# A graph convolution with residual and layer norm: which block of the first stage goes without a tile of g

## The chip, the cores and the metric

The kernel runs on one core of one Trainium2 chip. The metric is the device time of the program in microseconds, as the median of several executions. One more execution was recorded by the hardware profiler; every duration and every view in this document comes from such a profiled execution.

## The reference

The inputs are x (8 x 4096 x 256), a square matrix A (4096 x 4096, sparse and denser towards its first rows and columns) and a weight W (256 x 256), all float32. What is computed, cut to what matters:

```python
HW = jnp.einsum('bnf,fo->bno', H, W)                 # H is x
A_norm = jax.nn.relu((A + A.T) * 0.5)
D = jnp.sum(A_norm, axis=1)
d_inv_sqrt = jnp.where(D > 0, D_safe ** (-0.5), 0.0)
DAD = d_inv_sqrt[:, None] * A_norm * d_inv_sqrt[None, :]
L_norm = jnp.eye(N) - DAD
out = relu(jnp.einsum('nm,bmo->bno', L_norm, HW))
x = layernorm(x + out)                               # over the last axis
```

## The kernel before, in words

The kernel has two stages on the one core. The first stage makes two arrays in device memory: `a_dram`, the symmetrised and clipped matrix, and `g_dram`, the rows of x times W, each scaled by its node's r = D^(-1/2). The second stage gathers, for each pair of row tiles of the result, only the rows of these two arrays that are needed, multiplies them on the tensor engine (PE), and adds the residual and the layer norm.

The change is in the first stage. The matrix is cut into 8 x 8 blocks of 512 x 512, and the two loops run over the upper triangle: for row i from 0 to 7, for column j from i to 7. Off the diagonal a block (i, j) means two tiles, (i, j) and (j, i); on the diagonal one. So there are 36 blocks with 64 tiles. For each block the kernel

- loads the tiles, 1 MB each, on the queue of SyncE (SP), line 486, into a pool `adj` of four buffers;
- transposes the partner tile on PE in 16 pieces per tile (`symmetrise`, L496, tile `tr`) and adds it to the tile itself on VectorE (DVE), four additions per tile (L500, tile `sym`, a pool of three buffers);
- in `keep`, halves and clips the tile on ScalarE (ACT, L504), sums it in groups of 32 columns on DVE (L507, `sums`) and again (L512, `part`), notes on GpSimd (POOL, L508) which groups are not zero, and stores it into `a_dram` from ACT's queue (L513).

The tile (i, j) is spoken of as the first of the block and (j, i) as the second.

Beside most blocks stands one tile of g. There are 32 of them, of 128 nodes each. `form(m)` makes one: it loads x for these nodes in two halves (`xin`, L589 on SP's queue, or L555 on POOL's for rows 4 and up), transposes them on PE (L596, `xtr`), copies them out of PSUM on ACT (L597, `xt`), multiplies by W on PE (L607, `pg`) and scales by r on ACT while leaving PSUM (L617, `gt`). Then it stores the tile (L622) and has a small strip of `a_dram` loaded for it (`fetch`, POOL's queue). `multiply` uses both in the next block for the result's first row tile (L565, `lead`, 16 products).

A tile whose r is not known yet is kept unscaled: the last ten tiles (22 to 31) are made that way, one ahead of the loops and the others in rows 0 and 1. All others wait until `degrees(i)` at the end of a row has given r for the four tiles of that row; they stand in a list `known`. How many tiles of g a block takes is what `quota(i, j)` says: one off the diagonal, one on the diagonal from row 4 on, none on the diagonals of rows 0 to 3. Row 2 has six blocks, (2,2) to (2,7). At its start `known` holds tiles 4 to 7, and the ten early ones are used up. So blocks (2,3), (2,4), (2,5) and (2,6) take tiles 4, 5, 6 and 7, and (2,7) finds nothing to take, although its quota is one. Block (3,3), which follows, has a quota of none; (3,4) takes tile 8.

PSUM has eight banks: four belong to `lead` throughout the stage, and four (`b0`) turn over between the transposes, the tiles of g and the counts of the lists.

A third kind of work is spread over rows 2 to 5: the lists of which rows the second stage will gather (`patterns`, `count_place`, `more`, `count_place_rest`, later `spread_early` and `collect_index`). It is almost all small operations on DVE. A list `due` says after how many tiles each step comes; `run_due` counts down once for every tile kept. In row 2 these steps fall beside blocks (2,2) to (2,6), for the first of the second stage's units.

The order of instructions on each engine is not written by hand. The program gives the work in the order of the loops, and a scheduler in the framework puts it in an order per engine, by the operations' dependencies and its own estimate of their lengths. Each engine then runs its instructions in that order.

Of the kernel before, what the change touches and what calls it, by code (L numbers as in the profile page):

```python
# [67 lines left out]
def kernel(  # L68
# [402 lines left out]
    with (  # L471
# [175 lines left out]

        def quota(i, j):

            if i in (2, 3) and j == i:  # L650
                return 0
            return int(j > i or i > 3)

# [45 lines left out]
        for i in range(NS):  # L699
            diag = stat1.tile([P, A, P], F32, tag="diag", name=f"diag_{i}")  # L700
            for j in range(i, NS):
                tij = load_adj(i, j)
                tji = load_adj(j, i) if j > i else tij
                parts = [(i, j, tij, tji)] + ([(j, i, tji, tij)] if j > i else [])
                parts = [(p, spool.tile([P, A, S], F32, tag="sym", name=f"sym_{p[0]}_{p[1]}")) for p in parts]
                beside = [multiply(*args) for args in waiting]
                waiting.clear()
                products = len(beside)

                for _ in range(quota(i, j)):  # L710
                    if known:
                        beside.append(form(known.pop(0), True, i >= 4))
                    elif early:
                        beside.append(form(early.pop(0), False))
                for p, sym in parts:
                    for _ in symmetrise(*p, sym):
                        pass
                if i == NS - 1:


                    release_all(i - 1)
                    beside = beside[products:] + beside[:products]
                for n, b in enumerate(beside):
                    with tc.issue_after(done_pe[-1]) if i == NS - 1 and n < 2 else nullcontext():
                        for _ in b:
                            pass
                for (rows, cols, _, _), sym in parts:
                    keep(rows, cols, sym, diag)
                    run_due()
# [610 lines left out]
```

## Time and profile before

| | |
|---|---|
| median of three executions | 1734.53 us (1728.11 to 1739.32) |
| profiled execution, its own time | 1485.62 us |
| its span, first to last instruction | 1483.5 us |
| mean granted clock of PE | 0.975 |
| PE busy in the span | 1381.0 us, 93% |
| DVE busy | 1042.3 us, 70% |
| ACT busy | 361.0 us, 24% |
| bytes moved by DMA | 541.85 MB, 365 GB/s |
| PE busy in the first 560 us | 513.81 us |

The profiled execution is 249 us shorter than the median of the others. Its rows give the durations; its own time is what a sum of such durations is to be held against.

A row of a timeline reads: start in us from the beginning of the span, length in us, engine (PEld is the weight load of PE, and a q behind the name is the engine's queue), line, operation, what is written and read, the number of instructions merged into the row, and in brackets the idle time of the engine before it with what ended it. A row of a table by windows gives the stretch, its length, then the busy time of PE, PEld, DVE, ACT and POOL with the number of instructions, the granted clock of PE, the busy share of the DMA engines and the rate in GB/s.

### The profile page before, as it was taken

What the parts mean: (1) busy time and instruction counts of PE and PEld (TensorE: products, weight loads), DVE (VectorE), ACT (ScalarE), POOL (GpSimd) and SP (SyncE); (2) the same over time, 40 slices, a digit from 0 to 9 for tenths busy, and PEclk for the clock granted to TensorE, in tenths of its full rate; (3) what the DMA queues carried; (4) which work ended last, traced back from release to release, by engine and by line L of the source; (5) the groups of instructions that cost most, each with busy time, mean ns of one, the idle gap of its engine ahead of it and who ended that gap; (6) DMA issues with size and microseconds to landing.
All of it is one profiled execution on the core that took longest, in us unless ns stands there. A gap on an engine that the chain in (4) does not pass through costs nothing. (4 is left out here: it accounts for less than half of the span.)

```text
span 1483.5 us, 29574 instructions
## 1 busy us (share of the span) xinstructions
PE 1381.0 (93%) x10960; PEld 750.6 (51%) x10960; DVE 1042.3 (70%) x3174; ACT 361.0 (24%) x462; POOL 762.0 (51%) x1556
## 2 busy tenths in 40 slices
PE   7998988979999998999999999999989999988995
PEld 6777877757777773343433333333333344433432
DVE  4668569879687862219485897798889229999655
ACT  4555554434544460000101101101100010011111
POOL 2445010010223336775775767777777657677752
PEclk9999999999999999999999999999999999999997
DMA  9999999999999999999999999999999989999995
GB/s 347 365 370 385 402 363 360 387 384 328 352 361 349 370 387 377 391 400 334 368 381 359 375 396 367 392 387 378 347 379 386 401 293 360 334 346 400 394 364 188
DMA packets 216694, 541.85 MB, mean 365 GB/s; under 512 B 19070, under 2 KB 108862, under 8 KB 182110
## 3 DMA queue, kind: packets, MB, share of 16 engines
q0 software_dynamic: 55200, 282.68, 49.4%
q1 hardware_dynamic: 93200, 126.62, 24.7%
q10 hardware_dynamic: 68144, 130.58, 23.2%
q8 instruction: 89, 1.46, 0.4%
q14 instruction: 61, 0.50, 0.1%
HBM read 434.91 MB, written 136.34 MB: 385 GB/s over the span
## 5 line engine op out<-in xcount | busy, mean ns | idle before, releaser
L1175 PE MATMUL py<-g,ga 64*32 64x512 f32 (+1 forms) x7072 | 610.4, 607 | 24.5 <-DMA g<-g_dram,gi 24.2
L1175 PEld LDWEIGHTS py<-g,ga 64*32 64x32 f32 (+1 forms) x7072 | 226.9, 114 | 391.5 <-issue 313.9
L952 POOL DMA_INDIRECT ga<-a_dram,ai x265 | 287.6, 1085 | 134.0 <-PE py L1175 67.2
L960 POOL DMA_INDIRECT g<-g_dram,gi x265 | 294.0, 1110 | 112.2 <-issue 72.2
L768 ACT ACTIVATE y<-py,minus_r 128x512 f32<-128x512 f32 x120 | 72.7, 688 | 788.9 <-PE py L1175 570.0
L607 PE MATMUL pg<-w_sb,xt 128*128 128x256 f32 x1024 | 230.2, 384 | 4.3 <-ACT xt L597 4.3
L1175 PE MATMUL py<-g_hub,gh 128*128 128x512 f32 x496 | 229.5, 606 | 3.7 <-DVE pos_k L240 3.7
L607 PEld LDWEIGHTS pg<-w_sb,xt 128*128 128x128 f32 x1024 | 195.3, 193 | 30.4 <-ACT xt L597 5.0
L500 DVE TENSOR_TENSOR sym<-tr,adj 128x512 f32<-128x512 f32 x256 | 162.7, 682 | 58.4 <-PE tr L496 40.9
L507 DVE TENSOR_REDUCE sums<-sym 128x64 f32<-128x2048 f32 x64 | 145.3, 2279 | 62.4 <-ACT sym L504 62.4
L1175 PEld LDWEIGHTS py<-g_hub,gh 128*128 128x128 f32 x496 | 91.5, 191 | 136.2 <-issue 124.2
L496 PE MATMUL tr<-ident,adj 128*128 128x128 f32 x1024 | 136.2, 280 | 21.0 <-DVE sym L500 14.6
L504 ACT ACTIVATE sym<-sym 128x2048 f32<-128x2048 f32 x64 | 122.6, 1915 | 113.6 <-DVE sym L500 107.5
L508 POOL TENSOR_SCALAR uses<-sums 128x64 uint8<-128x64 f32 x64 | 24.8, 388 | 239.4 <-DVE sums L507 203.7
L496 PEld LDWEIGHTS tr<-ident,adj 128*128 128x128 f32 x1024 | 115.3, 143 | 53.5 <-DVE sym L500 32.5
L443 DVE TENSOR_SCALAR low<-lists 128x17 f32<-128x17 f32 (+8 forms) x14 | 2.5, 176 | 197.4 <-PE lists L431 197.4
L778 DVE TENSOR_TENSOR xr<-xr,y 128x2048 f32<-128x2048 f32 x31 | 70.9, 2286 | 54.6 <-ACT y L768 43.1
L596 PE MATMUL xtr<-ident,xin 128*128 128x128 f32 x512 | 72.9, 291 | 20.6 <-DVE sym L500 12.0
L811 DVE TENSOR_SCALAR xr<-xr,mv,root 128x256 f32<-128x256 f32 x248 | 85.8, 417 | 1.1
L787 DVE BATCH_NORM_STATS2 stats<-xr 128x6 f32<-128x256 f32 x248 | 84.0, 412 | 1.1
L565 PE MATMUL lead<-gt,strip 128*128 128x512 f32 x176 | 83.2, 594 | 0.0
L597 ACT COPY xt<-xtr 128x512 f32<-128x512 f32 x128 | 68.2, 592 | 59.2 <-PE xtr L596 57.6
(157 smaller groups left out, 1060.2 us busy)
## 6 DMA issues: line engine op xcount, KB each, us to landing
adj<-in_adj_dram SPq DMA_DIRECT2D x64, 1024.0 KB, 10.5
a_dram<-sym ACTq DMA_DIRECT2D x64, 1024.0 KB, 10.1
out_dram<-xr SPq DMA_DIRECT2D x31, 1024.0 KB, 25.1
xr<-in_x_dram ACTq DMA_DIRECT2D x28, 1024.0 KB, 20.4
xin<-in_x_dram SPq DMA_DIRECT2D x44, 512.0 KB, 11.1
g_dram<-gt ACTq DMA_DIRECT2D x22, 1024.0 KB, 9.4
xin<-in_x_dram POOLq DMA_DIRECT2D x20, 512.0 KB
g_dram<-held ACTq DMA_DIRECT2D x10, 1024.0 KB, 10.2
```

What stands on the lines that cost most here:

```text
L496: ins = nc.tensor.transpose(pt[:, c * P : (c + 1) * P], tji[:, c, a * P : (a + 1) * P], ident)
L500: nc.vector.tensor_add(sym[:, a, :], pt, tij[:, a, :])
L504: nc.scalar.activation(sym, sym, AF.Relu, scale=0.5)
L507: nc.vector.tensor_reduce(sums, sym.rearrange("p a (c q) -> p a c q", q=E), AX.X, ALU.add)
L565: nc.tensor.matmul(lead[c], lhsT=strip, rhs=g[:, c * S : (c + 1) * S], start=not done, stop=len(done) == NB - 1, skip_group_check=True,)
L596: nc.tensor.transpose(pt[:, k, c, :], xin[b // H][:, b % H + k, c * P : (c + 1) * P], ident)
L607: ins = nc.tensor.matmul(pg[:, k * FO : (k + 1) * FO], lhsT=xt[:, b + k, c, :], rhs=w_sb[:, c, :], start=(c == 0), stop=(c == FC - 1),)
L787: nc.vector.bn_stats(stats[:, b, :], z[:, b, :])
L811: nc.vector.tensor_scalar(z[:, b, :], z[:, b, :], mv[:, b, 0:1], rstd[:, b : b + 1], ALU.subtract, ALU.mult,)
L952: nc.gpsimd.indirect_dma_start(out=at if both else at[:, : E if one else P], out_offset=None, in_=a_pairs if both else a_groups if one els ...
L960: nc.gpsimd.indirect_dma_start(out=gt, out_offset=None, in_=g_dram, in_offset=bass.IndirectOffsetOnAxis(ap=gi[:, t : t + 1], axis=0), boun ...
L1175: return nc.tensor.matmul(py[2 * u + 1 + b][c][cols, :], lhsT=at[ps, off + cols.start : off + cols.stop], rhs=gt[ps, c * S : (c + 1) * S], ...
```

## The change

`quota` now names three blocks of rows 2 and 3 that take no tile of g: (2,2), (2,5) and (3,3). The two on the diagonal had none before. Block (2,5) is the fourth of row 2. With it left out, tile 6 goes to (2,6) and tile 7 to (2,7), so every tile of row 2 is still made in that row; the products of `lead` for each tile come one block later as well.

```diff
         def quota(i, j):

-            if i in (2, 3) and j == i:
+            if (i, j) in ((2, 2), (2, 5), (3, 3)):
                 return 0
             return int(j > i or i > 3)
```

## The prediction

> **What bounds the kernel now.** I read the page first, then the first stage by windows, then the stretch around the moved step as timelines of PE, VectorE (DVE) and ScalarE (ACT). A row carries no block number: blocks are told apart by counting rows in the built order.
>
> ```profile
> span 1483.5 us, 29574 instructions
> ...
> PE 1381.0 (93%) x10960; PEld 750.6 (51%) x10960; DVE 1042.3 (70%) x3174; ACT 361.0 (24%) x462; POOL 762.0 (51%) x1556
> ...
> DMA  9999999999999999999999999999999989999995
> ...
> a_dram<-sym ACTq DMA_DIRECT2D x64, 1024.0 KB, 10.1
> ```
>
> PE is busy for 93% of the span, and the DMA engines are at nine tenths or more in 38 of the 40 slices. The last row is a price used below: one store of a symmetrised tile takes 10.1 us from issue to landing. The first stage is the stretch up to some 560 us; seven windows of 80 us give PE 513.81 us of it. It is bound by PE and DMA together, so a moved step can only win where one of them stands still. The windows, with columns PE, PEld, DVE, ACT, POOL, granted clock, DMA share and GB/s, find one such place:
>
> ```profile
> 260.00:280.00 20.00, 18.80 (x107) 14.76 (x106) 19.26 (x49) 9.20 (x11) 1.10 (x3) 1.00 1.04 379
> 280.00:300.00 20.00, 20.00 (x113) 15.60 (x112) 14.06 (x29) 10.64 (x12) 0.73 (x2) 1.00 1.05 400
> 300.00:320.00 20.00, 11.15 (x65) 9.48 (x64) 17.29 (x28) 7.19 (x6) 5.39 (x12) 0.85 1.01 383
> ```
>
> From 300 to 320 us PE has 11.15 us of work in 20: that is 8.9 us lost. It is where block (2,7), which has no tile of g, meets (3,3), which has none either. Note too that DVE has 19.26 of 20 in the window where the change wants to put the light block. PE in that place:
>
> ```profile
> 297.63 2.74 PE L565 MATMUL lead<-gt,strip 128*128 128x512 f32 x6
> 300.21 1.91 PE L496 MATMUL tr<-ident,adj 128*128 128x128 f32 x16
> 307.77 3.95 PE L496 MATMUL tr<-ident,adj 128*128 128x128 f32 x20 [5.65 <-DMA adj<-in_adj_dram]
> 312.71 1.25 PE L496 MATMUL tr<-ident,adj 128*128 128x128 f32 x8 [0.99 <-DVE sym L500]
> 316.10 0.66 PE L496 MATMUL tr<-ident,adj 128*128 128x128 f32 x4 [2.13 <-DVE sym L500]
> 316.82 3.40 PE L596 MATMUL xtr<-ident,xin 128*128 128x128 f32 x16
> 320.01 2.34 PE L607 MATMUL pg<-w_sb,xt 128*128 128x256 f32 x8
> ```
>
> The waits are 5.65 + 0.99 + 2.13 = 8.77 us. The 5.65 has two causes within 0.2 us of each other: the second tile of (3,4), whose load was issued at 297.83 when (2,7) gave its buffer back, and DVE, which runs its queue in order:
>
> ```profile
> 300.85 0.69 DVE L500 TENSOR_TENSOR sym<-tr,adj 128x512 f32<-128x512 f32 x1 [0.99 <-PE tr L496]
> 301.46 4.46 DVE L507 TENSOR_REDUCE sums<-sym 128x64 f32<-128x2048 f32 x2
> ...
> 310.31 0.69 DVE L500 TENSOR_TENSOR sym<-tr,adj 128x512 f32<-128x512 f32 x1 [1.30 <-DMA a_dram<-sym]
> ```
>
> After a block without a tile of g, the two sums of that block (4.46 us) stand in front of the next block's additions, which free the PSUM banks; and the next-but-one tile needs the sym buffer whose store was issued at 299.87 and is released at 310.2. These two are the price of any light block.
>
> **The change part by part.** Nothing is removed or added: 32 tiles of g, the same bytes, the same buffers. Block (2,5) gives up tile 6, which goes to (2,6); tile 7 goes from (2,6) to (2,7). Per tile moved: 16 transposes L596 (1.91 us), 32 products L607 (7.07), 4 copies L597 and 4 scalings L617 on ACT, two xin loads on SP's queue, one g store on ACT's, one strip load on POOL's, and 16 lead products L565 in the next block (some 2.6 us of PE beside the transposes). The PE time in play is 1.91 + 7.07 = 9.0 us.
>
> *What goes.* The 8.77 us at 302 to 317: with tile 7's 9.0 us between (2,7) and (3,3), the loads of (3,4) go out at about 297 and land by 307, ahead of need, and DVE does (2,7)'s first sum under the products.
>
> *What comes, first at (2,6).* PE reaches it at 268.7 (end of the lead products), with 9.0 us fewer in front. DVE is not ready: the two sums of (2,5) end at 272.9 (268.44 + 4.47 in its timeline) and the small ones after them at 273.1, so (2,6)'s first four additions run 273.1 to 275.5. Its second tile needs the sym buffer of (2,5)'s first tile. In the built order that store is no longer behind the four xt copies, so it goes out right after the second relu starts, 268.1 (it was 270.68). With 10.1 us it lands at 278.2. Additions 278.4 to 280.9; the L596 transposes need the banks that these free and end at 281.5; L607 ends at 288.6. Then (2,7) begins at 288.7; before it was 293.2. So of 9.0 us the light block yields 4.5 and 4.5 is lost waiting.
>
> *At (2,7).* DVE now has list work in front: sum of (2,6) to 283.1, the list group (273.08 to 277.4 before, 4.3 us) to 287.5, the scan L236 that waits for PE's count at 288.9, the other sum (2.28) and small ones to 292.0. The additions take 5.8 us as before, to 297.8; tile 7's transposes end at 298.4, its products at 305.5.
>
> *At (3,3) and (3,4).* (3,3) on PE 305.5 to 307.6, lead to 310.2, (3,4) to some 314.6. The second relu of (2,7) stands behind the third scaling in ACT's order, near 304.5, so its store goes out at 306.5 and lands at 316.6. The second tile of (3,4) takes that buffer: its additions start at 316.6 where they started at 316.1. Tile 8's products start at 320 to 322 (a sum of 2.28 us stands between its additions in the new order); before, 320.0. Sum: 0 to +2, taken as **+1 us**.
>
> *Other queues.* SP: tile 7's second xin now stands behind the load for (3,3), which waits for (2,6)'s buffer, about 281; it lands near 291 and is wanted at 296. POOL: the strips of 6 and 7 are the same small loads, later; the degree work of row 2 (L524 to L536, some 2.5 us of DVE with the wait for POOL) now stands ahead of (3,3)'s additions, but under tile 7's products; without that cover it would cost 2.5. Beyond (3,4) the same instructions stand in nearly the same order, so the shift is carried on or absorbed.
>
> *Rule against row, the store.* The Trainium skill, "DMA: Bandwidth & Descriptors", section "Anatomy of one DMA — SWDGE (gpsimd) path", gives a DMA 2.0 us plus bytes over 436 GB/s (a fit for the other kind of queue): an estimate of 4.4 us for 1 MB. By it the store at 268.1 is in before it is wanted, (2,7) starts about 2.9 us sooner, the last store lands near 308, and tile 8's products start near 314.5: **-5.5 us**. The row says 10.1, and 299.87 to 310.2 in this very place, since both queues are full. I take the row.
>
> *Rule against row, the clock.* "TensorE: Matmul & The Clock Gate", section "HAM oscillation", says that idle gaps over some 3.4 us throttle PE. The rows agree: after a gap of 2.13 us (210.5 to 212.6) the 10 us window shows 1.00, after one of 4.03 (228.2 to 232.2) 0.83, and the window with the 5.65 us gap 0.85. By the rule, splitting this gap into waits near 3 us (276.1 to 279.1, and 314.6 to 317.3) would save the slow rows, at most 3.40 - 1.91 = 1.5 us, and the row L596 is also held by DVE. Bounds 0 and -1.5; I take 0, since both waits are close to the limit.
>
> *Bounds.* At best all 8.8 us of the old wait go and nothing comes: -8.8. At worst the 9.0 us uncovered at (2,6) are wholly lost and the old waits return at (3,4): +9.0.
>
> **Own time and the median.** The profiled execution took 1485.62 us (span 1483.5 and 2.1 around it); with the change 1486.6. The median shown is 1734.53, 1.168 times as long, and no view tells where these 249 us lie. If all stretch alike, +1 is +1.2, so **1735.7**, and the bounds are -10.3 and +10.5: within 1% (17.3 us, about what a measurement of this kernel can tell from no change) on both sides.
>
> **The rivals.**
> 1. *The gap is really closed.* Stores land in 4 to 7 us because the light block leaves the queues emptier. For it: SP issues nothing between 270.7 and 282.2. Against it: DMA share 1.04 there. Gain 5.5 to 8.8, times 1.168: **1724 to 1728**.
> 2. *VectorE becomes the bound* (slower). Place: (2,6) and (2,7), where it has 19.26 of 20 us already. Price: the 4.5 us still won at (2,6) are lost there, and the waits for stores come on top at (3,4), 4 to 9 us in all, times 1.168: **1739 to 1745**. It decides when stores land later than some 12 us or list work shifts further ahead of (2,7)'s additions. More than 1% slower needs the unprofiled runs to lose twice what the profile bounds.
> 3. *Waits in the unprofiled runs are much longer than here.* They are 249 us slower; if that time sits in first-stage waits, the same move could weigh 18 us or more either way. For it: nothing here excludes it. Against it: one block of 36.
> That the change does not do what it says is ruled out by the built order: tile 6's products stand after (2,6), tile 7's after (2,7).
>
> **How the numbers follow.** Forecast (-2 to +4 us): 0.45. Rival 1: 0.15. Rival 2: 0.15. Rival 3: faster 0.11, slower 0.14. So faster over 1% 0.11, within 1% 0.75, slower over 1% 0.14. The bounds give 1724 to 1745; the three runs lie 6.4 below and 4.8 above their median, and a second median scatters as well, so I add half as much again: 1714 to 1753. The forecast's own range is 1732 to 1740.
>
> **What would show it.** Right: PE's gap at 302 to 308 gone; a wait of some 6 us in all between 268.7 and 281.5; (2,7) from near 289; a second wait for a_dram<-sym on DVE near 316; tile 8's L607 at 320 to 322. Wrong: L607 of tile 8 before 317 (rival 1) or after 325 (rival 2); or a difference in the runs that the profiled spans don't show (rival 3).

## Result, and the profile after

The changed kernel took 1744.34 us (median of 22 runs, 1729.64 to 1756.44) against 1739.53 us for the kernel before on the same chip (22 runs, 1723.78 to 1754.55). The ratio is 1.002, with an interval of 0.9999 to 1.0041: no difference that these runs can tell from none, and at most some 7 us of loss. The forecast was a loss of 1.2 us.

Executions of these kernels lie on one of two levels, a short one of 1476 to 1488 us or a long one of 1712 to 1756 us, and the first trace of the kernel before is from the short level, the trace of the changed kernel from the long one:

```profile
span 1741.2 us, 29571 instructions
...
PE 1460.2 (84%) x10960; PEld 739.0 (42%) x10960; DVE 1042.2 (60%) x3174; ACT 361.2 (21%) x462; POOL 748.2 (43%) x1556
...
DMA  9999999999999996867777979779778668669984
```

DVE and ACT did the same work as before to 0.2 us. The DMA row shows where the two traces part: its nines, which ran through the first 32 slices before, end after 15 slices of 43.5 us, at 653 us, some 65 us behind the end of the first stage. So all comparisons of traces below are made inside the first stage, where the levels do not differ; the second stage is taken up further down.

The first stage by windows, in the changed kernel:

```profile
260.00:280.00 20.00, 13.41 (x71) 10.10 (x70) 16.60 (x29) 5.81 (x4) 0.75 (x3) 0.81 1.03 384
280.00:300.00 20.00, 19.97 (x111) 16.44 (x110) 17.70 (x47) 10.81 (x14) 1.04 (x2) 0.94 0.95 334
300.00:320.00 20.00, 17.07 (x100) 13.13 (x99) 15.20 (x28) 10.09 (x11) 5.42 (x12) 1.00 1.04 393
```

The hole from 300 to 320 us is gone: PE works 17.07 us there, not 11.15. But 260 to 280 fell from 18.80 to 13.41. Over the 60 us PE is busy 50.45 us, against 49.95 before, and gets through 282 instructions, against 285. The hole was not closed, it was moved and split. PE's timeline names the parts:

```profile
267.91 1.91 PE L496 MATMUL tr<-ident,adj 128*128 128x128 f32 x16
273.01 3.67 PE L496 MATMUL tr<-ident,adj 128*128 128x128 f32 x16 [3.18 <-DVE sym L500]
278.89 3.67 PE L596 MATMUL xtr<-ident,xin 128*128 128x128 f32 x16 [2.21 <-DVE sym L500]
282.36 7.12 PE L607 MATMUL pg<-w_sb,xt 128*128 128x256 f32 x32
...
298.35 7.07 PE L607 MATMUL pg<-w_sb,xt 128*128 128x256 f32 x32
...
315.13 1.25 PE L596 MATMUL xtr<-ident,xin 128*128 128x128 f32 x8 [0.73 <-DVE sym L500]
318.52 1.38 PE L596 MATMUL xtr<-ident,xin 128*128 128x128 f32 x8 [2.13 <-DVE sym L500]
319.74 8.76 PE L607 MATMUL pg<-w_sb,xt 128*128 128x256 f32 x32
```

The figures in brackets are the idle times: 3.18 + 2.21 + 0.73 + 2.13 = 8.25 us, where the old place had 8.77. The three L607 rows are tiles 6, 7 and 8. And DVE, on which all four waits end:

```profile
267.64 4.46 DVE L507 TENSOR_REDUCE sums<-sym 128x64 f32<-128x2048 f32 x2
...
272.28 2.47 DVE L500 TENSOR_TENSOR sym<-tr,adj 128x512 f32<-128x512 f32 x4
278.14 2.48 DVE L500 TENSOR_TENSOR sym<-tr,adj 128x512 f32<-128x512 f32 x4 [3.40 <-issue]
...
314.38 1.29 DVE L500 TENSOR_TENSOR sym<-tr,adj 128x512 f32<-128x512 f32 x2 [0.69 <-PE tr L496]
315.59 2.28 DVE L507 TENSOR_REDUCE sums<-sym 128x64 f32<-128x2048 f32 x1
317.78 0.68 DVE L500 TENSOR_TENSOR sym<-tr,adj 128x512 f32<-128x512 f32 x1
```

The first row holds the two sums of the light block (2,5), in front of the additions that free PE's banks; the third is the second tile of (2,6), 3.40 us late with DVE idle. The view gives no releaser for it ("issue"); what it waited for was settled by an experiment. The last three rows stand at (3,4): a sum of 2.28 us lies between the additions of its second tile, and PE waits its 2.13 us for the ones behind that sum. The kernel before has such a sum in this place too, at 313.17, and the same wait of 2.13.

### The profile page after: what moved, and what is told of

Its sections match the earlier page's. It is cut to its first block, busy times and chain, and to the rows that moved or that the text cites. A ratio compares the mean times of both kernels' runs of the same rounds, so it can differ in the third digit from the quotient of the medians.

```text
span 1741.2 us, 29571 instructions
## 1 busy us (share of the span) xinstructions
PE 1460.2 (84%) x10960; PEld 739.0 (42%) x10960; DVE 1042.2 (60%) x3174; ACT 361.2 (21%) x462; POOL 748.2 (43%) x1556
## 3 DMA queue, kind: packets, MB, share of 16 engines
q0 software_dynamic: 55200, 282.68, 43.5%
## 4 chain that ended last, share of the span: by engine, by line
PE 56%; another core or an unknown queue 12%; DVE 12%; DMA 9%; issue 5%; ACT 2%; POOL 2%; ACTq 0%; DVEq 0%; POOLq 0%
PE py L1175 39%; PE pg L607 8%; DMA a_dram<-sym 5%; PE tr L496 3%; DVE sym L500 3%; PE xtr L596 3%; PE lead L565 3%; DVE sums L507 1%; DMA ga<-a_dram,ai 1%; DVE stats L787 1%; DMA xin<-in_x_dram 1%; DVE xr L811 1%; POOL g L960 1%; POOL ga L952 1%
## 5 line engine op out<-in xcount | busy, mean ns | idle before, releaser
L1175 PE MATMUL py<-g,ga 64*32 64x512 f32 (+1 forms) x7072 | 682.5, 667 | 215.2 <-ACTq L1210 194.6
L1175 PEld LDWEIGHTS py<-g,ga 64*32 64x32 f32 (+1 forms) x7072 | 210.4, 120 | 669.2 <-ACTq L1210 357.4
L952 POOL DMA_INDIRECT ga<-a_dram,ai x265 | 273.2, 1031 | 279.6 <-PE py L1175 216.1
L607 PE MATMUL pg<-w_sb,xt 128*128 128x256 f32 x1024 | 230.5, 384 | 4.3 <-ACT xt L597 4.3
L607 PEld LDWEIGHTS pg<-w_sb,xt 128*128 128x128 f32 x1024 | 195.3, 193 | 30.9 <-ACT xt L597 5.0
L596 PE MATMUL xtr<-ident,xin 128*128 128x128 f32 x512 | 77.0, 301 | 23.7 <-DVE sym L500 16.9
L565 PE MATMUL lead<-gt,strip 128*128 128x512 f32 x176 | 83.6, 595 | 0.0
```

The source lines that it names most:

```text
L565: nc.tensor.matmul(lead[c], lhsT=strip, rhs=g[:, c * S : (c + 1) * S], start=not done, stop=len(done) == NB - 1, skip_group_check=True,)
L596: nc.tensor.transpose(pt[:, k, c, :], xin[b // H][:, b % H + k, c * P : (c + 1) * P], ident)
L607: ins = nc.tensor.matmul(pg[:, k * FO : (k + 1) * FO], lhsT=xt[:, b + k, c, :], rhs=w_sb[:, c, :], start=(c == 0), stop=(c == FC - 1),)
L952: nc.gpsimd.indirect_dma_start(out=at if both else at[:, : E if one else P], out_offset=None, in_=a_pairs if both else a_groups if one els ...
L1175: return nc.tensor.matmul(py[2 * u + 1 + b][c][cols, :], lhsT=at[ps, off + cols.start : off + cols.stop], rhs=gt[ps, c * S : (c + 1) * S], ...
```

## Experiments

Places in the first stage are counted from the start of the L607 products of tile 5 or of the last tile of g in row 1 (both lie ahead of the block (2,5)), so that a small shift at the start of a trace does not count. The expectations call that last tile of row 1 "tile 3"; by the order of the loops it is tile 31, one of those kept unscaled, and its way out of PSUM is the copy to `held` and not L617. It is the same place in every kernel, so no figure changes; below it is tile 31. The stage ends with the last product of `lead`. The four kernels of each of the first two comparisons ran once each with a profile; those of the third were timed as well, 14 to 22 times.

### The two kernels again

> The kernel before, profiled once more. It is to tell what of the difference between the two traces is scatter. From the start of tile 3's products (the last tile of g of row 1, the same in both kernels) the first trace has 105.0 us to the start of tile 8's products and 367.5 us to the end of the first stage. The theory (light block's gain is eaten by waits, nothing else is touched) expects 105 within 1 us again; for the end of the stage, scatter of some 5 us. The rival (the change delays the later rows as well) expects 367.5 within 2. The whole span: near 1740 us, as every timed run, not 1483.5 as in the first trace.

> The changed kernel, profiled once more. First trace: 105.5 us from tile 3's products to tile 8's, 373.2 us to the end of the first stage. The theory expects 105.5 within 1 us, and an end of the stage that falls within the scatter of the kernel before. The rival (the later rows are delayed by the change) expects 373 within 2, 5 to 6 us over the kernel before.

The kernel before took 1712.92 us and the changed one 1725.36; both on the long level. A third trace of the changed kernel came with the timed runs below. In us:

| | tile 5 to 6 | 5 to 7 | 5 to 8 | tile 8 to 9 | tile 8's 32 products | 31 to end of stage |
|---|---|---|---|---|---|---|
| before, first trace | 17.38 | 33.20 | 66.92 | 16.83 | 7.52 | 367.46 |
| before, again | 17.40 | 33.21 | 66.47 | 17.05 | 7.74 | 369.71 |
| changed, first trace | 30.09 | 46.08 | 67.46 | 19.10 | 8.76 | 373.17 |
| changed, again | 30.26 | 46.50 | 68.20 | 19.10 | 8.76 | 375.92 |
| changed, timed | 28.95 | 45.65 | 67.60 | 19.31 | 8.97 | 369.33 |

The two traces of before, one from each level, agree within 0.45 us up to tile 8: so up to there the levels make no difference. Tile 8 comes 0.5 to 1.7 us later with the change, as forecast. The next step, to tile 9, is 2.1 to 2.5 us longer in all three traces, which was not forecast. The rest of the stage, from tile 9 to its end, took 245.6 and 248.1 us in the kernel before and 248.6, 248.8 and 244.2 in the changed one: there the two cannot be told apart.

### The store that the second tile of (2,6) waits for

The store of (2,5)'s first tile is left out, and its place in `a_dram` is written with (5,2)'s, the second tile of the same block; the matrix that the second stage reads is therefore not the right one in that block. The number of bytes stays the same. (In this kernel the lines behind `keep` are numbered 5 higher.)

```diff
-            nc.scalar.dma_start(a_dram[...i, j...], sym)
+            if (i, j) != (2, 5):
+                nc.scalar.dma_start(a_dram[...i, j...], sym)
+            if (i, j) == (5, 2):
+                nc.scalar.dma_start(a_dram[...j, i...], sym)
```

> The changed kernel, with one thing taken away: the store of (2,5)'s first tile reads the second tile's buffer instead (same bytes, same place in memory, so that part of the stored matrix holds the other tile's values). So the sym buffer that (2,6)'s second tile takes waits for no store. The theory: the 3.4 us of VectorE before the second four additions of (2,6) go, tile 6's products start 2.5 to 3.4 us sooner, (2,7) too, and tile 8's products start 102 to 103.5 us after tile 3's instead of 105.5. The rival (the DMA engines are the bound, and what one wait gives is taken by the next): tile 6's products sooner, tile 8's at 105 to 106 as before.

DVE of this kernel, in the same place:

```profile
272.49 4.29 DVE L500 TENSOR_TENSOR sym<-tr,adj 128x512 f32<-128x512 f32 x7
```

and PE:

```profile
273.23 3.67 PE L496 MATMUL tr<-ident,adj 128*128 128x128 f32 x16 [3.18 <-DVE sym L500]
...
279.72 7.07 PE L612 MATMUL pg<-w_sb,xt 128*128 128x256 f32 x32
```

Seven additions now follow without a pause, so the 3.40 us were the store of (2,5)'s first tile. In the changed kernel it is the first of these two:

```profile
267.22 2.30 ACTq L513 DMA_DIRECT2D a_dram<-sym  x2
```

It was issued at 267.22 and waited for until 278.14, 10.9 us; in the other two traces of the changed kernel it was 11.3 and 10.3 us. PE's second wait is gone; its first, 3.18 us for the sums of the light block, stayed. Tile 6 came 27.25 us after tile 5 (changed: 29.8 in the mean of three), tile 8 65.61 (67.75): of the 2.5 us won at tile 6, 2.1 arrived at tile 8. From tile 31 it came at 103.65 us, close above the 102 to 103.5 expected; the rival's 105 to 106 fell. The time was 1720.32 us, which one run cannot tell from 1725.36.

### List work two tiles later

`count_place_rest` and its scan and dozen small DVE operations stand between the sums and additions of (2,7) in the changed kernel. Here they come two tiles later.

```diff
-                    due.append([at + 2 + 3 * gap, count_place_rest, (u,)])
+                    due.append([at + 2 + 3 * gap + (2 if i == 1 else 0), count_place_rest, (u,)])
```

On the changed kernel:

> The changed kernel with the last step of the first unit's lists (the scan at L236 and what follows) two tiles later, so that VectorE's additions of (2,7) no longer stand behind a scan that waits for PE's count. The theory: these additions start about 1.6 us sooner after PE reaches (2,7) (0.7 us after it instead of 2.9), tile 7's products 1 to 2 us sooner; the work comes back in front of (3,3), under tile 7's products, and tile 8's products start 104 to 105 us after tile 3's. The rival that has VectorE as the bound there: tile 8's products stay at 105.5 or come later, since the work is only moved.

On the kernel before:

> The kernel before with the last list step of the first unit two tiles later, as was done to the changed kernel. Changed kernel with it: tile 8's products 104.7 us after tile 3's, the end of the first stage 367.3 (before: 367.5 and 369.7). The theory (the step cost the changed kernel only because VectorE's additions stood behind a scan that waits for PE, while in the kernel before PE had just given that count when (2,7) came): no gain here, tile 8's products 104.5 to 107 us after tile 3's, later if anything, because the step now stands before (3,3) without a tile of g to cover it. The rival (the step is in the way in any order): 1 to 2 us sooner, 103 to 104.

On the changed kernel, 1711.76 us in its run, tile 8 came at 66.61 us from tile 5 (104.70 from tile 31, as expected): some 1.1 us sooner than in the mean of the changed kernel. Its PE row:

```profile
319.24 1.38 PE L596 MATMUL xtr<-ident,xin 128*128 128x128 f32 x8 [2.13 <-DVE sym L500]
320.45 7.07 PE L607 MATMUL pg<-w_sb,xt 128*128 128x256 f32 x32
```

The wait of 2.13 us is the same as in the changed kernel, but the products run in 7.07 us, not 8.76, which comes on top of the 1.1. That is the clock, seen in windows of 10 us. The changed kernel:

```profile
270.00:280.00 10.00, 4.78 (x21) 4.39 (x22) 6.60 (x11) 1.91 (x1) 0.73 (x2) 0.61 1.02 385
...
320.00:330.00 10.00, 10.00 (x40) 7.88 (x39) 2.88 (x4) 4.96 (x6) 0.37 (x1) 0.83 1.06 402
```

and the one with list work later:

```profile
320.00:330.00 10.00, 10.00 (x52) 8.18 (x52) 4.57 (x6) 5.54 (x7) 0.37 (x1) 1.00 1.06 405
```

PE is busy for all 10 us in both, and gets through 40 instructions in the one and 52 in the other, at a granted clock of 0.83 and 1.00.

On the kernel before the same edit ran in 1480.72 us beside 1486.24, on the short level. The theory, that it does little there (tile 8 at 104.5 to 107 from tile 31), fell, and the rival's 103 to 104 was met: tile 8 came at 103.78 where before had 104.99, and here too its products took 7.07 us instead of 7.52. The big gap had stayed:

```profile
306.27 3.72 PE L496 MATMUL tr<-ident,adj 128*128 128x128 f32 x20 [5.38 <-DMA adj<-in_adj_dram]
```

So up to the start of tile 8 the edit is worth about a microsecond on either kernel, wherever the light block is. At the start of tile 9 it is 1.2 us on the kernel before (82.5 us from tile 5 against 83.6) but 2.9 on the changed one (84.0 against 86.9), since there the slow products went as well; and at the end of the stage, from tile 31, it left nothing to see on the kernel before (367.5 us, against 367.5 and 369.7), while the changed one came in at 367.3 (against 369.3 to 375.9), in one trace each.

### Which block is the light one

```diff
-            if i in (2, 3) and j == i:
+            if (i, j) in ((2, 2), (2, 3), (3, 3)):     # or (2, 6) in place of (2, 3)
                 return 0
             return int(j > i or i > 3)
```

> The same change with another size: the block of row 2 without a tile of g is its second, (2,3), next to (2,2), which has none either. From tile 3's products to tile 8's products the kernel before has 104.5 to 105.0 us, the changed one 105.5 (108.0 in a trace that lost 1.9 us before the light block). The theory (a light block gives back about half of its 9 us because VectorE's sums and the store of a sym tile hold up the next block, and two light ones in a row give less): 106 to 110 us, slower than both. The rival (only the total of PE's and the DMA engines' work counts, the place does not): 105 within 1.

> The light block is the fifth, (2,6), so it lies apart from (3,3) by one block with a tile of g, as (2,5) lies by two. The theory: half of the 9 us is lost at (2,7), where VectorE's sums of (2,6), the scan that waits for PE's count and the wait for the store of (2,6)'s first tile meet; tile 8's products 105 to 107 us after tile 3's, within 1.5 of the changed kernel. The rival with the place indifferent: 105 within 1. The rival that VectorE's list work is what costs at (2,6): 102 to 104, since that work lies behind by then.

With (2,3) light, 1488.45 us beside 1486.24, tile 8 came at 110.68 us from tile 31, 5.7 us later than in the first trace of before and a little beyond the upper end expected. PE in this kernel:

```profile
228.57 1.97 PE L496 MATMUL tr<-ident,adj 128*128 128x128 f32 x8 [4.03 <-DVE sym L500]
...
235.94 2.82 PE L496 MATMUL tr<-ident,adj 128*128 128x128 f32 x12 [2.47 <-DVE pos_k L240]
...
316.63 1.12 PE L596 MATMUL xtr<-ident,xin 128*128 128x128 f32 x4 [5.31 <-DVE sym L500]
```

Block (2,2) has no tile of g either, so two light blocks meet here, as (2,7) and (3,3) do in the kernel before. The wait of 4.03 us was there before; 2.47 + 1.10 + 0.60 us come behind it (the last two ahead of rows not shown), and at (3,4) the 5.31 and one of 1.67 are left of 8.77. So 4.2 us of waits are paid and 1.8 won, which is 2.4 of the 5.7. Rows behind the waits ran slower too (tile 4's products 8.03 us, not 7.07); the rest was not taken apart.

With (2,6) light, 1487.86 us, tile 8 came at 104.43 from tile 31, near before, with one wait of PE at the block behind the light one:

```profile
294.39 4.23 PE L496 MATMUL tr<-ident,adj 128*128 128x128 f32 x20 [3.97 <-DVE pos_r L241]
```

No store was waited for there: DVE's second four additions followed with a pause of 0.77 us, and that for PE. The theory had asked for 105 to 107 and missed by a little; "the place is indifferent" (105 ± 1) fits. This trace also lost 1.6 us ahead of tile 5, and without that tile 8 would stand near 103, which the third reading asked for. The run does not decide.

### A diagonal block that takes a tile, so that no two light blocks meet

Here (3,3) takes tile 8; only (2,7) in front of it and, at the end of row 3, (3,7) are light.

```diff
-            if i in (2, 3) and j == i:
-                return 0
-            return int(j > i or i > 3)
+            return int(j > i or i > 2)
```

> The kernel before, but (3,3) takes a tile of g (tile 8), so that the light block (2,7) has none beside it, and the last block of row 3, (3,7), goes without one. From tile 3's products to tile 12's, in (4,4): before 175.5 to 175.9 us, changed kernel 179.7 to 181.7. The theory (a light block alone loses 4 to 5 us, the pair (2,7) and (3,3) lost 8.8 of PE): one light block here after (2,7) and one after (3,7), so 174 to 178. The rival (the pair is worse than two alone): 170 to 173.

It ran in 1475.65 us beside 1486.24. PE:

```profile
307.10 2.64 PE L596 MATMUL xtr<-ident,xin 128*128 128x128 f32 x12 [4.37 <-DVE sym L500]
309.53 7.72 PE L607 MATMUL pg<-w_sb,xt 128*128 128x256 f32 x32
```

One wait of 4.37 us is left of 8.77. Counted at tile 12, by which both kernels have made the same tiles, it is 8.0 us ahead (167.92 against 175.91 from tile 31). The theory (174 to 178, one light block is as dear as another) failed, and the rival (170 to 173) did not go far enough: up to tile 12 a pair of light blocks cost more than two that stand alone. One of the two, (3,7), lies close in front of tile 12, and a part of its price may fall behind it: one tile later, at tile 13, the lead was 6.2 us (186.15 against 192.31). At the end of the stage 4.1 us were left (363.34 against 367.46; 6.4 against the second trace of before). The remainder of the 10.6 us is not in the first stage, and it rests on one run of each.

### Timed runs

> The changed kernel timed against the kernel before on one chip. In the traces its first stage ends 3.5 to 6 us later, counted from tile 3's products, and what follows is the same. The theory: ratio 1.002 to 1.004. The rival (the difference in the traces is scatter): 0.999 to 1.001.

> The kernel before with tile 8 in (3,3) and (3,7) without one, timed. Its trace has tile 12's products 7.6 to 8.0 us sooner than the kernel before and the end of the first stage 4.1 to 6.4 us sooner. The theory (two light blocks in a row lose more than two apart): ratio 0.993 to 0.997. The rival (what is won is lost again before the second stage starts): 0.998 to 1.001.

> The same with the last list step of the first unit two tiles later as well. In the kernel before that step later made the span 4.7 us shorter on the same kind of chip, though the end of the first stage only 0 to 2 us. If the two add up: ratio 0.990 to 0.994. If the step only pays where two light blocks meet: the same as without it, 0.993 to 0.997.

> The changed kernel's light block (2,5), with tile 8 in (3,3), (3,7) without one, and the list step two tiles later. The theory (a light block alone loses 4 to 5 us wherever it stands, and neither of these two has one beside it): the same as with the light block at (2,7), ratio 0.990 to 0.997. The rival (the light block at (2,5) costs more, by the slow clock after its waits): 2 to 4 us slower than with (2,7).

`after_timed` is the changed kernel once more, `diag_timed` the kernel in which (3,3) takes tile 8, `diag_rest_later` that with the list work two tiles later, and `light_apart_rest_later` has (2,5) and (3,7) light, tile 8 in (3,3), and the list work later:

```diff
-            if i in (2, 3) and j == i:
+            if (i, j) == (2, 5):
                 return 0
-            return int(j > i or i > 3)
+            return int(j > i or i > 2)
```

The kernel before had 1738.03 us here (67 runs, 1722.91 to 1752.09).

| | median, us | ratio to before | interval | tile 31 to 12 | 31 to end of stage |
|---|---|---|---|---|---|
| `after_timed` | 1740.74 | 1.0018 | 0.9995 to 1.0041 | 178.58 | 369.33 |
| `diag_timed` | 1738.17 | 0.9980 | 0.9956 to 1.0004 | 168.11 | 366.67 |
| `diag_rest_later` | 1733.83 | 0.9965 | 0.9943 to 0.9986 | 171.30 | 366.29 |
| `light_apart_rest_later` | 1740.40 | 1.0022 | 0.9993 to 1.0051 | 175.64 | 369.05 |

The change again costs a little or nothing: a second interval that holds 1, and a ratio between what the theory and its rival had asked for, so this does not decide whether the difference in the traces is scatter. `diag_timed` was expected at 0.993 to 0.997, and the rival at 0.998 to 1.001: the rival's size it is, though the interval reaches into the other. The 10.6 us of the single run did not come again. Its lead of some 7.5 us at tile 12 is down to 0.8 to 3.0 us at the end of the stage, measured against the two traces of before. `diag_rest_later` fits what was expected if the gains do not add up. It is the only one of the four whose interval stays below 1, by 0.35%; its first stage ended no sooner than that of `diag_timed` (366.29 against 366.67), so where the gain lies is not shown. With the light block at (2,5) instead of (2,7) that was gone: the median is 6.6 us higher and the intervals do not meet. The theory (the place makes no difference, 0.990 to 0.997) fell; the rival had the direction, and 2 to 4 us. So in a second setting too, (2,5) is not a better place for a light block than (2,7).

## Why the prediction was right, and where it was not

**The size of the result.** A loss of 1.2 us was forecast, and that no difference would be told from the runs. The second held. The measured loss, 4.8 us between the medians, has an interval from about 0 to 7 us; it contains the 1.2 without showing it. The median of 1744.34 us itself lies above the forecast's own range of 1732 to 1740 and inside that of rival 2, but the kernel before had also moved, from 1734.53 with three runs to 1739.53 with 22. What can be held against the forecast are the traces.

**The chain at (2,6), right.** This trace is ahead by 0.8 us at tile 5; adding that to the times seen, the forecast points were met within 1.1 us, with one exception. First additions of (2,6): 273.1 forecast, 272.28 seen. Second ones: 278.4, seen 278.14. Tile 6's products: end 288.6, seen 289.48, which is the exception, 1.7 us late. Additions of (2,7): 292.0 to 297.8, seen 292.29 to 297.80. Tile 7's products: 298.4 to 305.5, seen 298.35 to 305.42. One term was too large: the light block was to yield 4.5 of its 9.0 us. From tile 5, (2,7) began 37.1, 37.5 and 36.7 us on in the three traces, where before had 40.2; that is a yield of 2.6 to 3.5. What is missing is about what slow rows behind the waits took: tile 6's transposes and products made 10.8 to 11.0 us together, where 9.0 had been put down. (The products of `lead` are eight for each tile in the traces, 3.6 us when they stand together, and not 16; no step of the working hangs on it.)

**The store, row against rule, right.** The row of 10.1 us was taken, against the estimate of 4.4 us from "DMA: Bandwidth & Descriptors", section "Anatomy of one DMA — SWDGE (gpsimd) path", in the Trainium skill. The measurement decides: 10.3 to 11.3 us in the three traces, and the run without that store put the whole wait on it. With 4.4 us it would have landed at 271.6, before DVE came to it at 274.75.

**The last store, wrong, without effect.** A second wait for a store was forecast near 316, with 10.1 us once more. The store went out at 306.25 (forecast 306.5):

```profile
306.25 0.37 ACTq L513 DMA_DIRECT2D a_dram<-sym  x1
```

But the additions began at 314.38 and had waited for PE alone: it landed in at most 8.1 us. Tile 8's transposes still waited 2.13 us, for the additions behind the sum at 315.59, and tile 8 came at 319.74, or 320.5 with the offset, inside 320 to 322. So the sum of 0 to +2 holds (0.5 to 1.7 seen), on a path that differs in its last step.

**The clock, mis-sized.** The term was taken as 0, with bounds of 0 and -1.5. The rows after the waits did stay slow, so nothing was saved; but both bounds lay on the side of a gain, and the slow rows turned out a loss. The 16 transposes behind the 3.18 us wait took 3.37 to 3.67 us in all three traces, not 1.91, although that wait is shorter than the 3.4 us which "TensorE: Matmul & The Clock Gate", section "HAM oscillation", in the Trainium skill gives as the limit. And a second slow stretch, behind the waits of 0.73 and 2.13 us, fell on tile 8's products: 8.76 to 8.97 us instead of 7.52 to 7.74, that is +1.2 us, with a clock of 0.83 in that window of the first trace.

**"Carried on or absorbed" beyond (3,4), mis-sized.** The step from tile 8 to tile 9 is +2.2 us in the mean. 1.2 of it are the clock. The other 1.0 lie between the end of tile 8's products and the start of tile 9's: 9.5 us in the first trace of before (327.36 to 336.83), 10.5 in the changed kernel (328.33 to 338.83). The scheduler's order on DVE differs there. In the kernel before a sum comes ahead of a tile's additions:

```profile
326.63 2.29 DVE L507 TENSOR_REDUCE sums<-sym 128x64 f32<-128x2048 f32 x1 [5.62 <-ACT sym L504]
```

In the changed kernel it stands between them, and PE's transposes, which need the banks, stretch: the row of 16 takes 2.56 us instead of 1.91.

```profile
329.72 0.67 DVE L500 TENSOR_TENSOR sym<-tr,adj 128x512 f32<-128x512 f32 x1
...
330.83 2.28 DVE L507 TENSOR_REDUCE sums<-sym 128x64 f32<-128x2048 f32 x1
...
333.77 0.69 DVE L500 TENSOR_TENSOR sym<-tr,adj 128x512 f32<-128x512 f32 x1
...
334.04 2.56 PE L496 MATMUL tr<-ident,adj 128*128 128x128 f32 x16
```

All three traces of the changed kernel have this order and 10.5 us, and the kernel with the list work later has both as well. That the order makes the difference was read from these rows and not tested apart. So the true sum up to tile 9 was about +3.3 us, not +1. The 4.8 and 2.7 us of the medians are of that size, but both intervals hold zero. At the end of the stage the means from tile 31 differ by 4.2 us (372.8 against 368.6); 3.3 of it are there at tile 9 already, 0.6 come from one trace that lost 1.8 us ahead of tile 5, and 0.3 arose behind tile 9, where traces of one kernel differ by 2.5 to 4.6.

**The 249 us, and rival 3.** They are not waits of the first stage. From the end of that stage to the end of the span, the first trace of before took 901.1 us, and its second, on the long level, 1126.1; the changed kernel 1153.8, 1130.5 and 1154.1. All traces on the short level, of whichever kernel, have 895 to 901. In the second stage it is the products of gathered rows that stretch. Their group in the first trace of before:

```profile
L1175 PE MATMUL py<-g,ga 64*32 64x512 f32 (+1 forms) x7072 | 610.4, 607 | 24.5 <-DMA g<-g_dram,gi 24.2
```

and in the changed kernel:

```profile
L1175 PE MATMUL py<-g,ga 64*32 64x512 f32 (+1 forms) x7072 | 682.5, 667 | 215.2 <-ACTq L1210 194.6
```

PE now stands idle 194.6 us for line 1210, an empty instruction on ACT by which two halves of PE's array take turns. In the second trace of before, with the same program, it is 153.4 us. So the level does not go with the kernel. All runs of one comparison were made on one chip, and the level was short on one chip and long on two others; a difference between chips is the nearest rival, and no run here put both levels on one known chip. (The changed kernel was seen on the long level only.) Rival 3, that waits in the first stage make the move weigh 18 us, has nothing left for it. Stretching the +1 by 1.168 was unfounded as well, since the first stage is about as long on both levels; it made 0.2 us of difference.

**Rivals 1 and 2.** The gap was not closed: 8.25 us of waits stand where 8.77 stood. Nor did DVE become the bound: PE's waits end on it, but it is busy 49.50 us of the 60 from 260 to 320, less than the 50.61 of before, and it stood idle for the store; tile 8 came at 319.74 and not after 325.

## What to carry to other kernels

When a step is made lighter so that a heavier one can fill a hole elsewhere, ask what the next step's buffers hang on. Here the light block at (2,5) took 9.0 us of PE's work away and moved the next block but one forward by only 2.6 to 3.5, because a queue that runs in order (two sums, 4.46 us) and a store of 10 to 11 us stood in front of the block behind it. What helped in the traces was to keep two light blocks from meeting. But an advance in the middle of a stage need not reach its end: 7.4 to 8.0 us at tile 12 became 0.8 to 6.4 at the end of the stage, and in the timed runs no difference clear of noise.

## What was not expected of the hardware

The two levels, some 250 us apart, differ in the second stage (895 to 901 us against 1126 to 1164) and hardly in the first. Why ACT's empty instruction comes late on the long one was not tried, and its cause stays open.

Waits of PE below 3.4 us were followed by a lower clock. Around a wait of 3.18 us in the changed kernel, the 10 us window showed 0.61. (The ends of PE's rows are modelled, so the distance of 3.18 from 3.4 is not to be leaned on.) But the length of a wait does not decide alone: behind one of 2.13 us in front of tile 8 the window had 0.83 in the changed kernel and 1.00 in the one with later list work. That one lacks the wait of 0.73 us just before; yet the kernel with (2,6) light has 0.67 and 2.13 us there, and its products took 7.07 us. What decides between them the runs do not show.
